# One copy of each node's row for both experts, in two row buffers, with the weight picked in the block

## The chip, the core and the metric

One core of a Trainium2 chip runs the whole kernel in one launch. The metric is the time of one execution on the device in microseconds (us), as a median of several runs. The engines are named as in the profile: PE (matmul; PEld is its weight load), DVE (vector), ACT (scalar/activation), POOL (GpSimd, which issues the gathers and scatters), and SP (SyncE, which issues the plain DMAs).

## The reference

The input is 6250 nodes of 256 features and 100000 edges of 96 features, sorted by target node `dst`. The kernel computes two layers, each with a residual around it:

```
x = x + gnn(layernorm(x))
    gnn(v): sums, maxima and means of the edges of each node
            h = relu(concat[v, sum, max, mean, u] @ W1 + b1) @ W2 + b2;  return h + v
x = x + ffn(layernorm(x))
    ffn(v): gate_logits = v @ gate_w + gate_b            # 16 experts
            the two best experts, weights softmax(their logits)
            each: relu(v @ w1[e] + b1[e]) @ w2[e] + b2[e]
            y = v + weighted sum;  return layernorm(y) * gamma + beta
```

## The kernel before

Node tiles have P = 125 nodes; there are 50, taken from the last to the first in 13 groups: group 0 has two tiles, the others four (GS = 4). The order of all work is written out by hand: `at_slot(T, function, ...)` puts a function at a slot, the slots are run through in order, and each engine gets its instructions in that order. A group has 12 slots (SLOTS); B = 12 g is the first slot of group g. Between the slots a stream of edge work (`steps`, lines 316 to 320) is laid on DVE by a time budget of 4.6 us a slot.

**First stage, by group.** For group g: edge rows are gathered by POOL (`take_edges` L722 and `take_carry` L729, from about slot B - 10), joined on DVE (`join_edges`, L735 and L737), masked on ACT (`mask_edges`, L742), turned on PE (`turn`, L755, copied out by ACT L756), and put through the MLP (`hidden` L766 and L771, `output` L779, eight slots and four slots). DVE adds the residual (`residual`, L784) and takes statistics. `find_block` and `take_blocks` (L490 to L495) find the edges' places by gathers of POOL. `chain_runs` carries runs over partitions on DVE (L395, L396, L438) and POOL writes them (`carry_d`, L440).

**Routing of a group.** `root_b` and `scale_b` give the scale of the second layer norm (`stat`); `norm_b` at slot B + 15 writes the normalized rows into the tile `xr` on ACT (L806); `turn_b` turns them on PE (L818), `logits` L826, `choose`, `rank` and `place` (slot B + 22) give each node its two experts, its two places in the row store `xg_d`, and its two weights; `send` (slots B + 23 and B + 24, two tiles each) scatters the rows with POOL's indirect DMA (L891), two DMAs a tile, eight a group. Each row has 256 features and 5 more numbers (DR = D + 5): its weight, the node with a mark for the later of the two, the place of the partner row, and the two numbers that undo the layer norm. `xr` holds two copies of each row, since weight, mark and partner differ, and there is one buffer of it (`xrp`, bufs=1).

**Last stage, by block.** A block is 256 rows of one expert. The first NA = 14 blocks are of one often chosen expert whose full blocks are known early; then `count_all` and `table_rest` work out the others, 43 blocks (b = 14 to 56). `load_block` (SP) loads the rows xb, the expert's weights wt (1026 KB) and its output bias eb, three buffers of weights, issued two blocks ahead. `run_block(b)` orders one block as follows: `weigh(b-1)` (DVE L1053 adds pY and xe to yb; ACT L1055 scales it by the row's weight; SP stores it in `y_d`), the load of b + 2, `finish(b-2)` (DVE L1093, L1094, then POOL's scatter L1096), the first half of the first matmuls (L1122, ACT L1128), `turn_block(b+1)` (PE L1036, copy xT, DVE L1041 for xe, and for b >= NA the indices from_i L1044 and to_i L1046), the second half, POOL's gather of the partner rows (`take_partners`, L1066), `stats_y(b-1)` (L1074 to L1089), and the second matmuls (L1142). The scale for a row is read straight from the loaded row:

```
nc.scalar.activation(yb[:, h, :], yb[:, h, :], AF.Copy, scale=xb[:, h, D:D + 1])
```

Of the kernel before, what the change touches and what calls it, by code (L numbers as in the profile page):

```python
# [9 lines left out]
F32 = mybir.dt.float32  # L10
# [9 lines left out]
P = 125  # L20
# [10 lines left out]
GS = 4  # L31
# [13 lines left out]
def kernel(  # L45
# [35 lines left out]
    WROW = B1O + FC  # L81
    NR = (2 * N - NE) // SB + NE
    NB = NA + NR
    DR = D + 5
    NG = (NT + GS - 1) // GS
    ER = EP * sum(JR)

# [104 lines left out]
    gtp = mlp.enter_context(tc.tile_pool(name="gt", bufs=2))  # L192
    sm = mlp.enter_context(tc.tile_pool(name="sm", bufs=2))
    xrp = mlp.enter_context(tc.tile_pool(name="xr", bufs=1))
    win0 = ExitStack()
    w0p = win0.enter_context(tc.tile_pool(name="win0", bufs=2))
    EP_ = {}
# [602 lines left out]

    def norm_b(g):
        a, z = GRP[g]
        G[g]["xr"] = xr = xrp.tile([P, GS, 2, DR], F32, name="xr")
        for i in range(z - a):
            t = a + i
            nc.scalar.activation(xr[:, i, :, 0:D], G[g]["xt"][:, i, None, :].to_broadcast([P, 2, D]), AF.Identity,  # L806
                                 scale=stat[:, 0, t:t + 1], bias=stat[:, 1, t:t + 1])
        n = z - a
        nc.scalar.copy(xr[:, :n, :, D + 3], stat[:, 2, a:z, None].to_broadcast([P, n, 2]))
        nc.scalar.copy(xr[:, :n, :, D + 4], G[g]["mvb"][:, :n, 0:1].to_broadcast([P, n, 2]))  # L810

    def turn_b(g, k):
        n = GRP[g][1] - GRP[g][0]
        if k == 0:
            G[g]["gT"] = gtp.tile([128, DC, GS * P], F32, name="gT", bufs=1)
        pT = pTp.tile([128, GS * P], F32, name="pT")
        for i in range(n):
            nc.tensor.transpose(pT[:, i * P:(i + 1) * P], G[g]["xr"][:, i, 0, k * 128:(k + 1) * 128], ident[:P, :P])  # L818
        nc.scalar.copy(G[g]["gT"][:, k, :n * P], pT[:, :n * P])

    def logits(g):
# [42 lines left out]
    def place(g):  # L864
        a, z = GRP[g]
        n, xr, mk, dv = z - a, G[g]["xr"], G[g]["mk"], G[g]["dv"]

        rk = gtp.tile([P, GS, NE], F32, name="rk")
        nc.vector.tensor_tensor(rk[:, :n], G[g]["pR"][:, :n * NE].rearrange("p (i e) -> p i e", e=NE),
                                erow[:, None, :].to_broadcast([P, n, NE]), op=OP.add)  # L870
        nc.vector.tensor_tensor(mk[:, :n], mk[:, :n], rk[:, :n, None, :].to_broadcast([P, n, 2, NE]), op=OP.mult)
        posf = gtp.tile([P, GS, 2], F32, name="posf")
        nc.vector.tensor_reduce(posf[:, :n], mk[:, :n], AX.X, OP.add)
        G[g]["pos"] = pos = xrp.tile([P, GS, 2], I32, name="pos_i", bufs=2)
        nc.vector.tensor_copy(pos[:, :n], posf[:, :n])

        w0 = gtp.tile([P, GS], F32, name="w0")
        nc.vector.tensor_scalar(w0[:, :n], dv[:, :n], 1.0, None, op0=OP.add)
        nc.vector.reciprocal(w0[:, :n], w0[:, :n])
        nc.vector.tensor_copy(xr[:, :n, 0, D], w0[:, :n])  # L880
        nc.vector.tensor_mul(xr[:, :n, 1, D], w0[:, :n], dv[:, :n])
        last = gtp.tile([P, GS, 2], F32, name="i2")
        nc.vector.tensor_tensor(last[:, :n], posf[:, :n, ::-1], posf[:, :n], op=OP.is_gt)
        nc.vector.scalar_tensor_tensor(xr[:, :n, :, D + 1], last[:, :n], float(2 * N),
                                       node_i[:, a:z, None].to_broadcast([P, n, 2]), op0=OP.mult, op1=OP.add)
        nc.vector.scalar_tensor_tensor(xr[:, :n, :, D + 2], last[:, :n], float(NE * N), posf[:, :n, ::-1],  # L886
                                       op0=OP.mult, op1=OP.add)

    def send(g, i):
        for k in range(2):  # L890
            d = nc.gpsimd.indirect_dma_start(out=xg_d[:, :],  # L891
                                             out_offset=IndirectOffsetOnAxis(ap=G[g]["pos"][:, i, k:k + 1], axis=0),
                                             in_=G[g]["xr"][:, i, k, :], in_offset=None)
# [26 lines left out]
    def open_experts():  # L920
        edges_until(len(JR) - 1)
        assert next(stream, None) is None
        edges.close()
        MB["pools"] = pools = ExitStack()
        for nm, bufs in (("tb", 1), ("wp", 3), ("xg", 6), ("bk", 3), ("yb", 4)):
            MB[nm] = pools.enter_context(tc.tile_pool(name=nm, bufs=bufs, side="right"))
        tb = MB["tb"]
        MB["half"] = half = tb.tile([128, 2], F32, name="half_i")
        nc.gpsimd.iota(half, pattern=[[-2 * N, 2]], base=0, channel_multiplier=-4 * N, allow_small_or_imprecise_dtypes=True)
        MB["tab_a"] = tb.tile([1, NA], I32, name="tab_a")  # L930
        MB["tab"] = tb.tile([1, 2, NR], I32, name="tab")
        MB["seen"] = tb.tile([128, NR], F32, name="seen")
        MB["more"] = tb.tile([1, 1], I32, name="more")
# [64 lines left out]
    def table_rest_2():  # L998
        pe = eps.tile([1, 2, NR], F32, name="ps")
        for k in range(2):  # L1000
            nc.tensor.matmul(pe[:, k, :], MB["er"][:, k:k + 1], ident[:NR, :NR], start=True, stop=True)
        nc.vector.tensor_copy(MB["tab"], pe)
        ps = pGp.tile([128, NR], F32, name="pg")
        nc.tensor.matmul(ps, MB["skip"].to_broadcast([NR, 128]), ident[:NR, :NR], start=True, stop=True)
        nc.vector.tensor_scalar(MB["seen"], ps, float(2 * N), None, op0=OP.mult)

    def open_final():
        mlp.close()
# [22 lines left out]
    def turn_block(b):  # L1031
# [7 lines left out]
        copy(xT, pX.rearrange("p k h r -> p k (h r)"))  # L1039
        BL[b]["xe"] = xe = MB["bk"].tile([128, 2, D], F32, name="xe")  # L1040
        nc.vector.tensor_tensor(xe, xb[:, :, 0:D], BL[b]["eb"][:, None, :].to_broadcast([128, 2, D]), op=OP.add)  # L1041
        if b >= NA:
            BL[b]["from"] = from_i = MB["xg"].tile([128, 2], I32, name="from_i")
            nc.vector.tensor_copy(from_i, xb[:, :, D + 2])  # L1044
            BL[b]["to"] = to_i = MB["xg"].tile([128, 2], I32, name="to_i")
            nc.vector.scalar_tensor_tensor(to_i, MB["half"], MB["seen"][:, b - NA:b - NA + 1], xb[:, :, D + 1],  # L1046
                                           op0=OP.add, op1=OP.max)

    def weigh(b):

        xb, xe = BL[b]["xb"], BL[b]["xe"]
        BL[b]["yb"] = yb = MB["yb"].tile([128, 2, D], F32, name="yb")
        nc.vector.tensor_tensor(yb, BL[b]["pY"], xe, op=OP.add)  # L1053
        for h in range(2):
            nc.scalar.activation(yb[:, h, :], yb[:, h, :], AF.Copy, scale=xb[:, h, D:D + 1])  # L1055
        r = BL[b]["r"]
        d = nc.sync.dma_start(y_d[ds(r, SB), :].rearrange("(p h) d -> p h d", h=2), yb.bitcast(I32))
        tc.declare_no_dep(d.ins, group="taken", reason="rows taken so far were written by earlier blocks")
# [13 lines left out]
    def stats_y(b):  # L1072
# [7 lines left out]
            nc.vector.bn_aggr(mv[:, h, :], bs)  # L1080
        BL[b]["z"] = z = MB["gy"].tile([128, 2, D], F32, name="z", bufs=3)
        for h in range(2):
            nc.scalar.activation(z[:, h, :], xb[:, h, 0:D], AF.Identity, scale=xb[:, h, D + 3:D + 4], bias=xb[:, h, D + 4:D + 5])
# [75 lines left out]
    def at_slot(T, fn, *a, cost=0.0):  # L1159
        tasks.append((T, len(tasks), fn, a, cost))  # L1160
# [21 lines left out]
    for g, (a, z) in enumerate(GRP):  # L1182
# [79 lines left out]

    def fill_rows():

        nc.vector.memset(fill[:, D + 1:], float(NE * N))
# [41 lines left out]
    cut_x = windows_of(xrp.tile([P, GS, 2, DR], F32, name="xr").rearrange("p i k d -> p (i k d)"), 1)[0]  # L1307
# [185 lines left out]
```

## Time and profile before

| | before |
|---|---|
| runs, median | 1313.23 us (1313.06, 1313.23, 1322.8) |
| profiled execution | 1304.08 us, span 1302.3 us |
| PE, PEld busy | 1134.1 us (87%), 788.7 us (61%) |
| DVE, ACT, POOL busy | 929.0 (71%), 646.4 (50%), 591.3 us (45%) |
| mean granted clock of PE | 0.947 |
| DMA | 260.99 MB, 200 GB/s |

| stretch, us | PE | DVE | ACT | POOL | clock | DMA share |
|---|---|---|---|---|---|---|
| 400 to 500 (groups) | 84.13 | 84.84 | 55.27 | 56.22 | 0.93 | 0.89 |
| 600 to 700 (groups) | 94.59 | 91.83 | 39.76 | 50.25 | 0.93 | 0.90 |
| 700 to 822 (groups, no edges left) | 120.09 | 54.30 | 47.54 | 40.11 | 1.00 | 0.31 |
| 822 to 900 (first blocks) | 74.15 | 32.52 | 21.57 | 17.07 | 0.98 | 0.25 |
| 1000 to 1100 (blocks) | 95.02 | 69.51 | 67.75 | 59.08 | 1.00 | 0.75 |
| 1100 to 1200 (blocks) | 97.85 | 71.51 | 69.76 | 58.04 | 1.00 | 0.77 |

The columns of the second table are busy microseconds in the stretch. The first activation of `norm_b` starts at 145.9, 205.2, 274.6, 327.5, 395.1, 462.7, 520.3, 579.1, 634.0, 692.3, 740.4, 789.7 and 835.4 us for groups 0 to 12. The first transposes of block 0 are at 820.50, those of block 14 at 937.65, of block 56 at 1265.51.

How to read the lines that follow. A line of the waits reads: engine, written tile and line, the releaser after the arrow, then the total wait in us, how often, and the longest. A line of a timeline reads: start in us, duration, engine, line, operation, written tile and read tiles, shapes, count, and in brackets the idle time of the engine before it with what ended it. In the slices each digit is the busy share of a fortieth of the span in tenths.

### The profile page before, as it was taken

The page shows a single profiled execution, that of the slowest core. Times are in us where ns is not written, and L with a number is a line of the kernel's source. Part 1 is how long each engine was busy: PE and PEld are TensorE (multiplying, and loading weights), DVE is VectorE, ACT ScalarE, POOL GpSimd, SP SyncE. Part 2 cuts the span into 40 slices and gives each one's busy share as a digit, 9 for nine tenths or more (in the row PEclk, how much of TensorE's full clock was granted, in tenths as well). Part 3 has the DMA queues.
Part 4 walks back from the last instruction along what each step waited for, and adds up shares of the span by engine and source line. Part 5 has one row for each costly group of instructions (what it writes and reads, how often), then busy time and mean ns, then how long its engine had stood idle before and what let it go on. Part 6 is the DMA issues. An engine that isn't in the chain of part 4 may idle for free.

```text
span 1302.3 us, 16684 instructions
## 1 busy us (share of the span) xinstructions
PE 1134.1 (87%) x4631; PEld 788.7 (61%) x4631; DVE 929.0 (71%) x2465; ACT 646.4 (50%) x1484; POOL 591.3 (45%) x731
## 2 busy tenths in 40 slices
PE   2494899879888879999999999997999999999992
PEld 1262365536545444646465565886888888888882
DVE  4569888869996989989999441444347767776764
ACT  3394256444637452533435333221266766676663
POOL 4122254563466654383643450303046656555664
PEclk9897799889998989989989999998999999999997
DMA  5948876795888897879988311222366777878771
GB/s 161 217 103 237 212 231 183 202 273 149 237 213 260 230 289 192 245 202 257 262 245 241 105 50 62 65 66 81 120 230 223 257 253 262 278 246 270 268 271 70
DMA packets 179473, 260.99 MB, mean 200 GB/s; under 512 B 35915, under 2 KB 145963, under 8 KB 173729
## 3 DMA queue, kind: packets, MB, share of 16 engines
q1 hardware_dynamic: 140241, 202.11, 52.0%
q0 software_dynamic: 39008, 57.22, 15.5%
q8 instruction: 40, 0.66, 0.2%
q14 instruction: 72, 0.59, 0.1%
q10 hardware_dynamic: 112, 0.41, 0.1%
HBM read 146.59 MB, written 121.88 MB: 206 GB/s over the span
## 4 chain that ended last, share of the span: by engine, by line
PE 30%; DMA 8%; DVE 7%; issue 3%; ACT 3%; SPq 2%; POOL 2%; DVEq 0%; POOLq 0%; ACTq 0%
PE acc L1122 9%; PE acc L1142 9%; PE acc L771 6%; DMA eb<-in_eb_dram 5%; PE acc L779 3%; POOL xg_d L891 1%; DMA xt<-in_x_dram 1%; DVE yb L1053 1%; PE pT L1036 1%; ACT yb L1055 1%; DMA rows_d<-rw 1%; DVE bsc L1079 1%; DMA cg<-carry_d,next_i 1%; DVE z L1089 1%; ACT hb L1128 1%
## 5 line engine op out<-in xcount | busy, mean ns | idle before, releaser
L771 PE MATMUL acc<-inT,w1x 128*128 128x500 f32 (+1 forms) x832 | 374.3, 601 | 0.0
L771 PEld LDWEIGHTS acc<-inT,w1x 128*128 128x128 f32 x832 | 162.7, 203 | 184.1 <-issue 182.2
L891 POOL DMA_INDIRECT xg_d<-xr,pos_i x100 | 133.4, 1334 | 241.1 <-DVE xr L886 177.6
L1122 PE MATMUL acc<-xT,wt 128*128 128x256 f32 x912 | 223.9, 389 | 15.2 <-ACT hb L1128 13.6
L1142 PE MATMUL acc<-wt,hb 128*128 128x256 f32 x912 | 206.8, 380 | 0.0
L1122 PEld LDWEIGHTS acc<-xT,wt 128*128 128x128 f32 x912 | 169.8, 192 | 45.9 <-ACT hb L1128 23.0
L1142 PEld LDWEIGHTS acc<-wt,hb 128*128 128x128 f32 x912 | 173.9, 191 | 23.9
L779 PE MATMUL acc<-w2s,hT 128*125 128x256 f32 x800 | 183.6, 386 | 0.0
L773 ACT ACTIVATE hT<-acc,c 128x500 f32<-128x500 f32 (+1 forms) x104 | 68.5, 658 | 226.2 <-PE acc L771 226.0
L779 PEld LDWEIGHTS acc<-w2s,hT 128*125 128x125 f32 x800 | 150.7, 192 | 22.8 <-issue 0.9
L1096 POOL DMA_INDIRECT out_dram<-g,to_i x86 | 95.7, 1113 | 104.2 <-ACT xT L1039 73.0
L1066 POOL DMA_INDIRECT g<-y_d,from_i x86 | 89.9, 1046 | 88.4 <-DVE to_i L1046 51.8
L495 POOL DMA_INDIRECT gb<-in_dst_dram,blk_i x50 | 67.9, 1359 | 131.1 <-DVE blk_i L492 77.6
L1128 ACT ACTIVATE hb<-acc,wt 128x256 f32<-128x256 f32 x200 | 87.9, 465 | 51.7 <-PE acc L1122 51.7
L1055 ACT ACTIVATE yb<-yb,xb 128x256 f32<-128x256 f32 x114 | 51.7, 501 | 103.1 <-DVE yb L1053 101.7
L316 DVE TENSOR_TENSOR rw<-rw,keep 125x768 f32<-125x768 f32 x81 | 77.2, 953 | 11.3 <-DMA rows_d<-rw 9.8
L319 DVE TENSOR_TENSOR rw<-rw,raw 125x768 f32<-125x768 f32 x88 | 83.4, 948 | 0.3 <-DMA raw<-in_edge_dram 0.3
L320 DVE TENSOR_TENSOR rw<-rw,raw 125x768 f32<-125x768 f32 x88 | 83.6, 950 | 0.0
L317 DVE TENSOR_TENSOR rw<-rw,bar 125x768 f32<-125x768 f32 x81 | 82.1, 1013 | 0.0
L756 ACT COPY inT<-pT 128x500 f32<-128x500 f32 (+1 forms) x65 | 35.9, 553 | 89.6 <-PE pT L755 89.5
L722 POOL DMA_INDIRECT at<-rows_d,first_i x44 | 62.5, 1420 | 37.6 <-issue 19.0
L1041 DVE TENSOR_TENSOR xe<-xb,eb 128x512 f32<-128x512 f32 x57 | 39.4, 691 | 55.7 <-DMA eb<-in_eb_dram 55.7
(301 smaller groups left out, 1633.5 us busy)
## 6 DMA issues: line engine op xcount, KB each, us to landing
wt<-in_wpack_dram SPq DMA_DIRECT2D x44, 1026.0 KB
rows_d<-rw SPq DMA_DIRECT2D x46, 960.0 KB
rows_d<-rw SPq DMA_DIRECT2D x46, 540.0 KB
raw<-in_edge_dram SPq DMA_DIRECT2D x46, 480.0 KB
xb<-xg_d SPq DMA_DIRECT2D x57, 261.0 KB
y_d<-yb SPq DMA_DIRECT2D x57, 256.0 KB
raw<-in_edge_dram SPq DMA_DIRECT2D x46, 270.0 KB
xt<-in_x_dram SPq DMA_DIRECT2D x12, 500.0 KB
```

The costliest lines, as they stand in the source:

```text
L316: nc.vector.tensor_tensor(su, prev[0], keep[c][:, :, s + j, None].to_broadcast(bcast), op=OP.mult)
L317: nc.vector.tensor_tensor(mx, prev[1], bar[c][:, :, s + j, None].to_broadcast(bcast), op=OP.min)
L319: nc.vector.tensor_tensor(su, su, x_j, op=OP.add)
L320: nc.vector.tensor_tensor(mx, mx, x_j, op=OP.max)
L771: nc.tensor.matmul(pH[:, :n * P], w1x[:, k, ms], inT[:, k, :n * P], start=False, stop=(k == KC - 1))
L779: nc.tensor.matmul(pO, G[g]["hT"][m][:, i * P:(i + 1) * P], w2s[:, m, :], start=(m == 0), stop=(m == HC - 1))
L891: d = nc.gpsimd.indirect_dma_start(out=xg_d[:, :], out_offset=IndirectOffsetOnAxis(ap=G[g]["pos"][:, i, k:k + 1], axis=0), in_=G[g]["xr"][ ...
L1066: d = nc.gpsimd.indirect_dma_start(out=g[:, h, :].bitcast(I32), out_offset=None, in_=y_d[:, :], in_offset=IndirectOffsetOnAxis(ap=BL[b]["f ...
L1096: d = nc.gpsimd.indirect_dma_start(out=out[:, :], out_offset=IndirectOffsetOnAxis(ap=BL[b]["to"][:, h:h + 1], axis=0), in_=g[:, h, :], in_ ...
L1122: nc.tensor.matmul(pB[i][:, half, :], wt[:, k * FF + m * 128:k * FF + (m + 1) * 128], xT[:, k, :], start=(k == 0), stop=(k == DC - 1))
L1128: nc.scalar.activation(hb[:, m, :], pB[i][:, half, :], AF.Relu, bias=bias)
L1142: nc.tensor.matmul(pY[:, h, :], hb[:, m, h * 128:(h + 1) * 128], wt[:, W2O + m * D:W2O + (m + 1) * D], start=(m == order[0]), stop=(m == o ...
```

## The change

A row gets 7 more numbers instead of 5, the same for both experts: both weights (D, D + 1), the second place (D + 2), the sum of both places (D + 3), the node (D + 4), and the two numbers of the layer norm. Both sends of a tile take the same copy. The tile holds two groups, `xr2[:, g % 2]`. The block works out by itself which weight is its own: it compares the second place with the row's own place (`at`, a table made once from the block table by one more pair of matmuls and an addition), gets the partner's place as sum minus own, and from the order of the two the mark that was sent before. In the first 14 blocks, whose expert has the lowest places, a comparison with N is enough. The sends of groups 0 to 9 are put one slot later. All places of the cleared rows are set to a larger number so that the new arithmetic leaves them out.

```diff
-    DR = D + 5
+    DR = D + 7
...
+    xr2 = xrp.tile([P, 2, GS, DR], F32, name="xr")
...
     def norm_b(g):
-        G[g]["xr"] = xr = xrp.tile([P, GS, 2, DR], F32, name="xr")
+        G[g]["xr"] = xr = xr2[:, g % 2]
         for i in range(z - a):
-            nc.scalar.activation(xr[:, i, :, 0:D], G[g]["xt"][:, i, None, :].to_broadcast([P, 2, D]), AF.Identity,
+            nc.scalar.activation(xr[:, i, 0:D], G[g]["xt"][:, i, :], AF.Identity,
                                  scale=stat[:, 0, t:t + 1], bias=stat[:, 1, t:t + 1])
-        nc.scalar.copy(xr[:, :n, :, D + 3], stat[:, 2, a:z, None].to_broadcast([P, n, 2]))
-        nc.scalar.copy(xr[:, :n, :, D + 4], G[g]["mvb"][:, :n, 0:1].to_broadcast([P, n, 2]))
+        nc.scalar.copy(xr[:, :n, D + 4], node_i[:, a:z])
+        nc.scalar.copy(xr[:, :n, D + 5], stat[:, 2, a:z])
+        nc.scalar.copy(xr[:, :n, D + 6], G[g]["mvb"][:, :n, 0])
...
     def place(g):
-        w0 = gtp.tile([P, GS], F32, name="w0")
-        nc.vector.tensor_scalar(w0[:, :n], dv[:, :n], 1.0, None, op0=OP.add)
-        nc.vector.reciprocal(w0[:, :n], w0[:, :n])
-        nc.vector.tensor_copy(xr[:, :n, 0, D], w0[:, :n])
-        nc.vector.tensor_mul(xr[:, :n, 1, D], w0[:, :n], dv[:, :n])
-        last = gtp.tile([P, GS, 2], F32, name="i2")
-        nc.vector.tensor_tensor(last[:, :n], posf[:, :n, ::-1], posf[:, :n], op=OP.is_gt)
-        nc.vector.scalar_tensor_tensor(xr[:, :n, :, D + 1], last[:, :n], float(2 * N), ...)
-        nc.vector.scalar_tensor_tensor(xr[:, :n, :, D + 2], last[:, :n], float(NE * N), ...)
+        w0, w1 = xr[:, :n, D], xr[:, :n, D + 1]
+        nc.vector.tensor_scalar(w1, dv[:, :n], 1.0, None, op0=OP.add)
+        nc.vector.reciprocal(w0, w1)
+        nc.vector.tensor_mul(w1, w0, dv[:, :n])
+        nc.vector.tensor_copy(xr[:, :n, D + 2], posf[:, :n, 1])
+        nc.vector.tensor_add(xr[:, :n, D + 3], posf[:, :n, 0], posf[:, :n, 1])
...
     def send(g, i):
-                                             in_=G[g]["xr"][:, i, k, :], in_offset=None)
+                                             in_=G[g]["xr"][:, i, :], in_offset=None)
...
     def table_rest_2():
-        ps = pGp.tile([128, NR], F32, name="pg")
-        nc.tensor.matmul(ps, MB["skip"].to_broadcast([NR, 128]), ident[:NR, :NR], start=True, stop=True)
+        ps = pGp.tile([128, 2, NR], F32, name="pg")
+        for k, of in enumerate((MB["skip"], MB["er"][:, 1:2])):
+            nc.tensor.matmul(ps[:, k], of.to_broadcast([NR, 128]), ident[:NR, :NR], start=True, stop=True)
+        nc.vector.tensor_tensor(MB["at"], ps[:, 1, :, None].to_broadcast([128, NR, 2]),
+                                MB["pair"][:, None, :].to_broadcast([128, NR, 2]), op=OP.add)
...
     def turn_block(b):
-        if b >= NA:
-            BL[b]["from"] = from_i = MB["xg"].tile([128, 2], I32, name="from_i")
-            nc.vector.tensor_copy(from_i, xb[:, :, D + 2])
-            BL[b]["to"] = to_i = MB["xg"].tile([128, 2], I32, name="to_i")
-            nc.vector.scalar_tensor_tensor(to_i, MB["half"], MB["seen"][:, b - NA:b - NA + 1], xb[:, :, D + 1],
-                                           op0=OP.add, op1=OP.max)
+        w0, w1, pos1, both, node = (xb[:, :, D + k] for k in range(5))
+        BL[b]["w"] = w = MB["xg"].tile([128, 2], F32, name="w_b")
+        if b < NA:
+            nc.vector.scalar_tensor_tensor(w, pos1, float(N), w1, op0=OP.is_ge, op1=OP.add)
+            nc.vector.tensor_tensor(w, w, w0, op=OP.min)
+            return
+        own = MB["at"][:, b - NA]
+        nc.vector.tensor_tensor(w, pos1, own, op=OP.not_equal)
+        nc.vector.tensor_add(w, w, w1)
+        nc.vector.tensor_tensor(w, w, w0, op=OP.min)
+        other, late = (MB["xg"].tile([128, 2], F32, name=nm) for nm in ("other", "late"))
+        nc.vector.tensor_sub(other, both, own)
+        nc.vector.tensor_tensor(late, other, own, op=OP.is_gt)
+        BL[b]["from"] = from_i = MB["xg"].tile([128, 2], I32, name="from_i")
+        nc.vector.scalar_tensor_tensor(from_i, late, float(NE * N), other, op0=OP.mult, op1=OP.add)
+        nc.vector.scalar_tensor_tensor(late, late, float(2 * N), node, op0=OP.mult, op1=OP.add)
+        BL[b]["to"] = to_i = MB["xg"].tile([128, 2], I32, name="to_i")
+        nc.vector.scalar_tensor_tensor(to_i, MB["half"], MB["seen"][:, b - NA:b - NA + 1], late, op0=OP.add, op1=OP.max)
...
     def weigh(b):
-            nc.scalar.activation(yb[:, h, :], yb[:, h, :], AF.Copy, scale=xb[:, h, D:D + 1])
+            nc.scalar.activation(yb[:, h, :], yb[:, h, :], AF.Copy, scale=BL[b]["w"][:, h:h + 1])
...
-            at_slot(B + SLOTS + 11 + i // 2, send, g, i)
+            at_slot(B + SLOTS + (12 if g < NG - 3 else 11) + i // 2, send, g, i)
```

More of the change, by code (lines that the diff above doesn't have):

```diff
@@ L817, in turn_b @@
         for i in range(n):
-            nc.tensor.transpose(pT[:, i * P:(i + 1) * P], G[g]["xr"][:, i, 0, k * 128:(k + 1) * 128], ident[:P, :P])
+            nc.tensor.transpose(pT[:, i * P:(i + 1) * P], G[g]["xr"][:, i, k * 128:(k + 1) * 128], ident[:P, :P])
         nc.scalar.copy(G[g]["gT"][:, k, :n * P], pT[:, :n * P])
@@ L875, in place @@
         nc.vector.tensor_copy(pos[:, :n], posf[:, :n])
-        w0 = gtp.tile([P, GS], F32, name="w0")
-        nc.vector.tensor_scalar(w0[:, :n], dv[:, :n], 1.0, None, op0=OP.add)
-        nc.vector.reciprocal(w0[:, :n], w0[:, :n])
-        nc.vector.tensor_copy(xr[:, :n, 0, D], w0[:, :n])
-        nc.vector.tensor_mul(xr[:, :n, 1, D], w0[:, :n], dv[:, :n])
-        last = gtp.tile([P, GS, 2], F32, name="i2")
-        nc.vector.tensor_tensor(last[:, :n], posf[:, :n, ::-1], posf[:, :n], op=OP.is_gt)
[L884 to L887, printed above, removed]
+        w0, w1 = xr[:, :n, D], xr[:, :n, D + 1]
[4 more added lines that the diff above has]
+        nc.vector.tensor_add(xr[:, :n, D + 3], posf[:, :n, 0], posf[:, :n, 1])
     def send(g, i):
@@ L931, in open_experts @@
         MB["tab"] = tb.tile([1, 2, NR], I32, name="tab")
+        MB["pair"] = pair = tb.tile([128, 2], F32, name="pair_i")
+        nc.gpsimd.iota(pair, pattern=[[1, 2]], base=0, channel_multiplier=2, allow_small_or_imprecise_dtypes=True)
         MB["seen"] = tb.tile([128, NR], F32, name="seen")
+        MB["at"] = tb.tile([128, NR, 2], F32, name="at_row")
         MB["more"] = tb.tile([1, 1], I32, name="more")
@@ L1002, in table_rest_2 @@
         nc.vector.tensor_copy(MB["tab"], pe)
-        ps = pGp.tile([128, NR], F32, name="pg")
-        nc.tensor.matmul(ps, MB["skip"].to_broadcast([NR, 128]), ident[:NR, :NR], start=True, stop=True)
-        nc.vector.tensor_scalar(MB["seen"], ps, float(2 * N), None, op0=OP.mult)
+        ps = pGp.tile([128, 2, NR], F32, name="pg")
+        for k, of in enumerate((MB["skip"], MB["er"][:, 1:2])):
+            nc.tensor.matmul(ps[:, k], of.to_broadcast([NR, 128]), ident[:NR, :NR], start=True, stop=True)
+        nc.vector.tensor_scalar(MB["seen"], ps[:, 0], float(2 * N), None, op0=OP.mult)
+        nc.vector.tensor_tensor(MB["at"], ps[:, 1, :, None].to_broadcast([128, NR, 2]),
+                                MB["pair"][:, None, :].to_broadcast([128, NR, 2]), op=OP.add)
     def open_final():
@@ L1041, in turn_block @@
         nc.vector.tensor_tensor(xe, xb[:, :, 0:D], BL[b]["eb"][:, None, :].to_broadcast([128, 2, D]), op=OP.add)
-        if b >= NA:
-            BL[b]["from"] = from_i = MB["xg"].tile([128, 2], I32, name="from_i")
-            nc.vector.tensor_copy(from_i, xb[:, :, D + 2])
-            BL[b]["to"] = to_i = MB["xg"].tile([128, 2], I32, name="to_i")
-            nc.vector.scalar_tensor_tensor(to_i, MB["half"], MB["seen"][:, b - NA:b - NA + 1], xb[:, :, D + 1],
-                                           op0=OP.add, op1=OP.max)
+        w0, w1, pos1, both, node = (xb[:, :, D + k] for k in range(5))
[16 more added lines that the diff above has]
+        nc.vector.scalar_tensor_tensor(to_i, MB["half"], MB["seen"][:, b - NA:b - NA + 1], late, op0=OP.add, op1=OP.max)
     def weigh(b):
-        xb, xe = BL[b]["xb"], BL[b]["xe"]
+        xe = BL[b]["xe"]
         BL[b]["yb"] = yb = MB["yb"].tile([128, 2, D], F32, name="yb")
@@ L1082, in stats_y @@
         for h in range(2):
-            nc.scalar.activation(z[:, h, :], xb[:, h, 0:D], AF.Identity, scale=xb[:, h, D + 3:D + 4], bias=xb[:, h, D + 4:D + 5])
+            nc.scalar.activation(z[:, h, :], xb[:, h, 0:D], AF.Identity, scale=xb[:, h, D + 5:D + 6], bias=xb[:, h, D + 6:D + 7])
         nc.scalar.activation(rs, mv[:, :, 1], AF.Sqrt, bias=eps_t)
@@ L1263, in fill_rows @@
     def fill_rows():
-        nc.vector.memset(fill[:, D + 1:], float(NE * N))
+        nc.vector.memset(fill[:, D + 1:], 4.0 * NE * N)
         for h in range(SB // 128):
@@ L1306 @@
     w1u = wk.tile([P, GS, D], F32, name="xn", bufs=1).rearrange("p i d -> p (i d)")[:GF, 0:HID]
-    cut_x = windows_of(xrp.tile([P, GS, 2, DR], F32, name="xr").rearrange("p i k d -> p (i k d)"), 1)[0]
+    cut_x = windows_of(xr2.rearrange("p k i d -> p (k i d)"), 1)[0]
     cut_w = w2s[:P].rearrange("p k d -> p (k d)")[:, 0:WE * EF].rearrange("p (k f) -> p k f", f=EF)
```

## The prediction

> **What bounds the kernel now.** Each view in turn. First the page's slices: which engine is full where.
>
> ```profile
> PE   2494899879888879999999999997999999999992
> DVE  4569888869996989989999441444347767776764
> DMA  5948876795888897879988311222366777878771
> ```
>
> A slice is 32.6 us. Up to slice 21 (700 us) DVE and PE are both nearly full: DVE folds edges, PE runs the node MLP. From 700 to 822 PE is alone and full (118.99 of 120 us at clock 1.00). From 905 to 1290 the 43 blocks of the chosen experts run, with PE, DVE and DMA all busy. The change touches the first stage and the last, so I priced each by itself.
>
> Second, the list of waits, for the step that the change rebuilds and for what runs next to it.
>
> ```profile
> DVE xe L1041 <- DMA eb<-in_eb_dram: 55.7, 36, 3.7
> DVE yb L1053 <- PE acc L1142: 52.2, 39, 2.9
> DVE at L735 <- DMA cg<-carry_d,next_i: 37.7, 10, 10.3
> PE pT L818 <- ACT xr L806: 30.0, 18, 10.3
> ACT xr L806 <- DMA at<-rows_d,first_i: 26.9, 3, 13.3
> ```
>
> L806 is norm_b's first activation of a group. With one buffer it cannot write before the eight row sends (L891) of the group before have landed; the releaser printed is only the DMA that came last by the records. The starts of L806 show real waits of ACT in groups 2, 4, 5, 6 and 9: 9.5, 11.2, 13.3, 2.3 and 4.0 us, and PE, whose transposes L818 follow, idles 6.5, 8.2, 10.3, 0 and 1.0 us.
>
> Third, the timelines of group 5's stall and of what came after it.
>
> ```profile
> 453.42 1.43 POOL L891 DMA_INDIRECT xg_d<-xr,pos_i  x1 [0.21 <-issue]
> 462.71 2.93 ACT L806 ACTIVATE xr<-xt,stat 125x512 f32<-125x512 f32 x4 [13.29 <-DMA at<-rows_d,first_i]
> 463.57 0.47 PE L818 MATMUL pT<-ident,xr 125*128 125x125 f32 x1 [10.27 <-ACT xr L806]
> 466.07 1.44 POOL L729 DMA_INDIRECT cg<-carry_d,next_i  x1 [0.30 <-issue]
> 474.56 3.48 DVE L735 SCALAR_TENSOR_TENSOR at<-cg,cross,at 125x96 f32<-125x96 f32 x1 [4.66 <-DMA cg<-carry_d,next_i]
> 488.13 0.44 ACT L742 ACTIVATE at<-at,ne_n 125x192 f32<-125x192 f32 x1
> 488.24 0.71 PE L755 MATMUL pT<-ident,at 125*128 125x125 f32 x4
> ```
>
> Read downwards: PE loses 10.3 us at 463, but at 488.24 it needs the edge sums of group 7, and these come just then, from the mask on ACT (488.13) after the join on DVE (474.56) after a gather on POOL (466.07) that stands in POOL's queue behind gathers and sends. Groups 4 and 6 meet in the same way (L755 at 299.96 with a wait of 0.69 on L742; at 421.35, beside the last L742 at 421.10). So PE's stall is slack against the join, and POOL's queue plus DVE set the end of the stage. The residual adds (L784) say the same: in groups 2 to 9 they start 3 to 12 us after PE has finished (L779), so DVE is the late one.
>
> Last, a block of the last stage.
>
> ```profile
> 1023.95 0.69 DVE L1041 TENSOR_TENSOR xe<-xb,eb 128x512 f32<-128x512 f32 x1 [1.19 <-DMA eb<-in_eb_dram]
> 1024.56 0.16 DVE L1044 CAST from_i<-xb 128x2 int32<-128x2 f32 x1
> 1024.63 0.22 DVE L1046 SCALAR_TENSOR_TENSOR to_i<-half_i,seen,xb 128x2 int32<-128x2 f32 x1
> 1024.76 0.69 DVE L1074 TENSOR_TENSOR g<-yb,g 128x512 f32<-128x512 f32 x1
> 1028.28 0.69 DVE L1053 TENSOR_TENSOR yb<-acc,xe 128x512 f32<-128x512 f32 x1 [0.30 <-PE acc L1142]
> 1056.53 0.69 DVE L1041 TENSOR_TENSOR xe<-xb,eb 128x512 f32<-128x512 f32 x1 [3.59 <-DMA eb<-in_eb_dram]
> 1060.48 0.68 DVE L1053 TENSOR_TENSOR yb<-acc,xe 128x512 f32<-128x512 f32 x1
> 1062.52 0.70 PE L1122 MATMUL acc<-xT,wt 128*128 128x256 f32 x2 [1.99 <-ACT hb L1128]
> ```
>
> An undisturbed block takes PE 7.53 us. DVE waits for eb, runs a chain of 3.95 us at least from xe to the next yb, and then is ready 0.30 us before PE's product: almost no slack. When eb lands late (1056.53) yb is late, ACT's scaling and hb stand behind it, and PE stalls for 1.99 us (1062.52 is yb + 2.04, as in the blocks around). This is where a longer DVE chain hurts.
>
> **The change, part by part.**
>
> *Two row buffers.* In the built order norm_b's first activation of a group waited on all eight semaphores of POOL's DMA queue; now it waits for DVE's statistics, and its activations for lanes of sends two groups back, which landed some 50 us before. So the five waits go, 40.3 us of ACT and 26.0 us of PE. What is late next is the join, at the three places above: PE would arrive some 10 us early and wait there. On the path I count only what the join itself gains: the carry write, which moves ahead of the last four sends in two groups, ends a 2.3 us wait of DVE at 275 (L395), the gathers behind a lane may leave 1.5 us sooner at 274, and L490 waits 1.4 us at 407 for an ACT that stood behind L806. These partly overlap: -2 us; bounds 0, and -26.0 with the half-rate time below if PE were the bound after all. Group 9 comes after the last gather wait: -1.0 us.
>
> The row on the clock: in 450 to 472, around group 5's stall, PE was granted 0.77 of its clock, in 385 to 410 0.73, in 265 to 285 0.83, against 1.00 from 700 to 820. I estimate some 8 us of PE time lost at half rate after the three stalls.
> [...]
>
> *Sends one slot later.* On POOL only the two carry writes change place. The second one waits for ct of L438, ready at 318.0, while the fourth send ends near 313.6: the last four sends and the gathers behind them start up to 4 us later. Joins of that group follow at 345.8, so cover is there; without it, 4 us. Counted 0.
>
> *place.* From pos_i (876.97) to the end of L886 (878.24) DVE took 1.27 us for seven small operations; the five that are left, at 0.19 us from start to start where one needs the other and 0.08 where not, end 0.48 us sooner. DVE is the late engine up to group 10: 11 x 0.48 = -5.3 us; bounds 0 (all reabsorbed by gathers) and -6.2 (13 groups).
>
> *norm_b on ACT.* 50 activations of 0.80 us become ones of 256 columns, 0.59 by L706's row: 10.5 us less, one more small copy of 0.19 a group. ACT is 40 to 57% busy there and nobody waits but L818: 0; without that cover -0.8 us a group.
>
> *Blocks.* Between xe and g stand two small operations (0.20 us); now eight, seven of them in dependent runs: 0.20 + 0.20 + 0.08 + five of 0.20 + 0.13 us against 0.20. The start-to-start of dependent small operations is that of L993 to L918, 0.18 to 0.24 us. So +1.2 us (bounds 0.6, if they start 0.08 apart, and 1.4).
> [...]
>
> In 40 blocks (b = 17 to 56) DVE's slack before yb ranges from 0 (12 blocks) to 0.9 us and adds up to 20.2 us. Delays add up to 40 x 1.2 - 20.2 = 27.8 us. A late yb(b-1) holds back, through SP's queue (y_d store, then xb, wt and eb for b+2), the eb that yb(b+1) needs: the loop spans two blocks, so a delay is paid once per two: +13.9 us. Bounds +4 (0.6 us) and +27.8 (paid in each block). Behind the delayed yb stand ACT's scaling and hb, hence PE; take_partners has from_i a block ahead of need.
>
> *Star blocks, table, bytes.* Two operations in each of 14 blocks: DVE waits 2.6 to 2.9 us for PE there: 0; without that, 0.28 each. One more pair of matmuls (0.31) and an addition (about 0.25) before the table's yb: +0.6. Rows of 8 bytes more: 0.1% of 261 MB: 0.
>
> **Sum:** -2 - 1.0 - 5.3 + 13.9 + 0.6 = +6.2 us. The profiled execution took 1304.08 us (span 1302.3), so 1310.3 by it; the runs' median is 1313.23, 9 us above it, and I add the same difference: **1319.4 us**, +0.5%. Differences under 1% (13 us) can hardly be told from none by these runs.
>
> **The rivals.**
> A: the waits pay in full. For: 26.0 us of idle PE and the clock. Against: the join rows. -26 - 8 in place of -3 and -5.3, blocks +14.5: 1293.7 us, 1.5% faster.
> B, on the slower side: the delayed yb is paid in each block, not in every second. It decides once eb lands over 10.0 us after yb(b-3), as in nearly all 40 blocks, and when each block's load also waits on its neighbour. For: SP's queue is in order. Against: an undisturbed DVE round is 6.0 + 1.2 = 7.2 us, under 7.53. +27.8 + 0.6 - 8.3: 1333.3 us, 1.5% slower.
> C: it doesn't do what it says, norm_b still waits (for lanes shared with later gathers). The built order speaks against it. -5.3 + 14.5: 1322.4 us.
>
> **How the numbers follow.** Forecast 0.47, A 0.14, B 0.33, C 0.06. Forecast and C lie within 1%: 0.53; A gives faster 0.14, B slower 0.33. The range goes from 1300 (join gains a third of PE's waits) to 1335 (B with its bound), leaving most of A out.
>
> **What would show it.** Right: L806's waits on DMA gone, PE's idle time moved before L755 or L766, the span up to block 0 about 8 us shorter, about 1.2 us more from xe to g, and block pitch up by some 0.35 us. Wrong: block 0 over 20 us earlier (A), a mean pitch over 8.3 us (B), or L806 still waiting (C).

## The result, and the profile after

The changed kernel takes 1330.5 us (median of 17 runs, 1323.8 to 1342.4); the kernel before takes 1313.1 us on the same chips (17 runs, 1305.5 to 1322.8). The ratio is 1.015, 95% interval 1.0124 to 1.0177: 1.5% slower, some 17 to 20 us. The forecast was 1319.4 us with a range of 1300 to 1335, so the time lies in the range, but the loss is about three times the +6.2 us of the sum and near the price of rival B.

Each kernel was profiled twice. The table gives the start of three additions yb on VectorE (L1053 before, L1068 after): block 0 is the end of the first stage, 16 to 56 are the blocks that the prediction summed over.

| | time of that execution | yb of block 0 | yb of block 16 | yb of block 56 | 16 to 56 | mean pitch |
|---|---|---|---|---|---|---|
| before | 1304.08 | 830.3 | 966.8 | 1281.3 | 314.5 | 7.86 |
| before, again | 1310.66 | 830.3 | 968.5 | 1288.3 | 319.7 | 7.99 |
| after | 1332.15 | 827.9 | 965.9 | 1309.9 | 343.9 | 8.60 |
| after, again | 1332.27 | 831.0 | 968.1 | 1310.2 | 342.1 | 8.55 |

The first profile of before comes from an execution 9 us under its median, and both of after lie 2 us above theirs, so the difference between the profiles (25 us on average) is larger than that of the medians. The picture is plain all the same: the first stage ends where it did, within the 3 us by which two profiles of one kernel differ, and everything is lost in 40 blocks.

The page's slices of the changed kernel, to be laid beside those of before:

```profile
PE   2494899879896969799999999998998998988883
DVE  4569889879986989899987414444487777777675
DMA  5948868785988897978995231122666767767762
```

In the last ten slices, which are blocks, PE shows 8 in six where before had 9 in all but the last, and DVE 7 nearly throughout where before had 7 and 6: more VectorE work per block, and a PE that waits.

The list of waits of the changed kernel, with the idle us, the times and the longest:

```profile
DVE yb L1068 <- PE acc L1157: 40.2, 24, 3.2
DVE at L736 <- DMA cg<-carry_d,next_i: 37.7, 9, 12.8
PE acc L1137 <- ACT hb L1143: 34.0, 32, 3.0
DVE xe L1044 <- DMA eb<-in_eb_dram: 31.4, 26, 4.0
PE pg L862 <- DVE mm L853: 25.5, 6, 10.5
```

Three things are to be seen. norm_b's wait on a DMA (L807 now) is gone from the list, and PE's 30.0 us ahead of its transposes with it; but 25.5 us stand at L862, the next place where PE needs VectorE. VectorE's wait for PE ahead of yb has shrunk from 52.2 us in 39 blocks to 40.2 in 24: its slack is used up. And PE now waits 34.0 us for hb in 32 blocks (13.6 in 14 before).

Group 5 in the changed kernel's timelines, first PE's line, then VectorE's, then PE's again:

```profile
457.01 0.59 PE L820 MATMUL pT<-ident,xr 125*128 125x125 f32 x4
476.08 2.60 DVE L736 SCALAR_TENSOR_TENSOR at<-cg,cross,at 125x96 f32<-125x96 f32 x1 [4.01 <-issue]
488.23 0.22 DVE L853 TENSOR_TENSOR mm<-mk 125x64 f32<-125x64 f32 x1
488.50 0.68 PE L862 MATMUL pg<-mm,before 125*125 125x64 f32 x2 [10.47 <-DVE mm L853]
489.60 0.63 PE L756 MATMUL pT<-ident,at 125*128 125x125 f32 x2
```

PE transposes group 5's rows at 457.0, where before it waited until 463.6. Then it runs dry 10.47 us long, because rank's mask (L853) stands in VectorE's queue behind the join (L736), which is no earlier than before (476.08 against 474.56). The transposes of the edge sums start at 489.60; before it was 488.24. The stall of 10.3 us has become one of 10.5 us, 25 us later.

A late block in VectorE's timeline and the matmuls of PE that follow:

```profile
1242.42 0.69 DVE L1044 TENSOR_TENSOR xe<-xb,eb 128x512 f32<-128x512 f32 x1 [4.01 <-DMA eb<-in_eb_dram]
1243.03 0.15 DVE L1052 TENSOR_TENSOR w_b<-xb,at_row 128x2 f32<-128x2 f32 x1
1244.27 0.22 DVE L1062 SCALAR_TENSOR_TENSOR to_i<-half_i,seen,late 128x2 int32<-128x2 f32 x1
1244.41 0.69 DVE L1089 TENSOR_TENSOR g<-yb,g 128x512 f32<-128x512 f32 x1
1247.55 0.68 DVE L1068 TENSOR_TENSOR yb<-acc,xe 128x512 f32<-128x512 f32 x1
1249.58 3.66 PE L1137 MATMUL acc<-xT,wt 128*128 128x256 f32 x8 [3.03 <-ACT hb L1143]
```

From xe to yb it is 5.13 us with no idle time but 0.36 us for the root (the square root that ScalarE takes); that is the shortest chain of the changed kernel, against 3.95 before. PE's product had been ready since 1243.9, and PE starts its second half 2.03 us after yb, after a stall of 3.03 us. Its eight matmuls then take 3.66 us where an undisturbed block takes 1.99. The windows around them say why (us of the window, busy times of PE, PEld, DVE, ACT and POOL, the granted clock, DMA share, GB/s):

```profile
1249.50:1252.90 3.40, 3.32 (x8) 2.66 (x9) 3.12 (x14) 1.35 (x4) 2.27 (x3) 0.51 0.43 147
1252.90:1257.00 4.10, 4.10 (x21) 3.61 (x20) 1.70 (x7) 2.73 (x6) 2.52 (x6) 0.99 0.86 274
```

For 3.4 us after the stall PE was granted half its clock. Blocks 16 to 56 of before had no such window in either profile.

**Where the time of a block goes.** In every profile, PE's second half starts 2.04 us after the yb before it, the last matmul of the product 5.08 us later and the next yb at the earliest 0.41 us later: 7.53 us. What a block takes beyond this is one of three things, which can be read off block by block: VectorE is still busy when PE's product is ready; or VectorE is idle and PE's release comes late all the same; or the 5.08 us are longer, at half clock. Added up from yb 16 to yb 56 (0 stands for less than 0.6; where a yb is late for both of the first two reasons, the split between them is good to some 0.6 us in a sum):

| kernel | 16 to 56 | PE, 40 x 7.53 | VectorE late | PE's release late | half clock |
|---|---|---|---|---|---|
| before; again | 314.5; 319.7 | 301.2 | 13.4; 18.8 | 0; 0 | 0; 0 |
| after; again | 343.9; 342.1 | 301.2 | 29.3; 31.6 | 8.7; 0 | 4.6; 9.1 |
| one buffer | 347.2 | 301.2 | 32.5 | 4.2 | 9.0 |
| small operations before xe | 322.0 | 301.2 | 18.2 | 1.1 | 1.2 |
| loads before store | 305.5 | 301.2 | 2.2 | 1.1 | 0 |
| both; again | 303.7; 303.5 | 301.2 | 2.4; 2.2 | 0 | 0 |
| before, six operations more | 331.5 | 301.2 | 23.1 | 4.4 | 2.7 |
| before, twelve operations more | 367.8 | 301.2 | 53.9 | 0 | 12.7 |
| before, loads first; again | 303.5; 303.5 | 301.2 | 2.2; 2.2 | 0 | 0 |

The 2.2 to 2.4 us of VectorE in the last rows are one block, the last, which is as late in nearly every profile. The 1.1 us in the row of the loads before the store are late releases inside two blocks, 34 and 48, at clock 1.00.

### The profile page after: what moved, and what is told of

Its sections match the earlier page's. It is cut to its first block, busy times and chain, and to the rows that moved or that the text cites. A ratio compares the mean times of both kernels' runs of the same rounds, so it can differ in the third digit from the quotient of the medians.

```text
span 1330.3 us, 16956 instructions
## 1 busy us (share of the span) xinstructions
PE 1136.9 (85%) x4633; PEld 796.3 (60%) x4633; DVE 970.2 (73%) x2726; ACT 637.4 (48%) x1497; POOL 589.1 (44%) x732
## 4 chain that ended last, share of the span: by engine, by line
PE 24%; DVE 11%; DMA 9%; issue 4%; ACT 3%; SPq 3%; POOL 0%; DVEq 0%; POOLq 0%; ACTq 0%
PE acc L1157 8%; PE acc L1137 8%; DMA eb<-in_eb_dram 5%; PE acc L772 4%; PE acc L780 3%; DMA rows_d<-rw 3%; DVE yb L1068 2%; ACT yb L1070 1%; DMA xt<-in_x_dram 1%; ACT hb L1143 1%; SPq L176 1%; DVE z L1104 1%; DVE rw L321 1%; DVE bsc L1094 1%; DVE g L1089 1%
## 5 line engine op out<-in xcount | busy, mean ns | idle before, releaser
L772 PE MATMUL acc<-inT,w1x 128*128 128x500 f32 (+1 forms) x832 | 365.4, 590 | 0.0
L772 PEld LDWEIGHTS acc<-inT,w1x 128*128 128x128 f32 x832 | 159.1, 198 | 178.4 <-issue 176.0
L1137 PE MATMUL acc<-xT,wt 128*128 128x256 f32 x912 | 229.2, 396 | 35.8 <-ACT hb L1143 34.0
L1137 PEld LDWEIGHTS acc<-xT,wt 128*128 128x128 f32 x912 | 172.7, 195 | 69.5 <-ACT hb L1143 45.3
L780 PE MATMUL acc<-w2s,hT 128*125 128x256 f32 x800 | 189.7, 395 | 0.0
L780 PEld LDWEIGHTS acc<-w2s,hT 128*125 128x125 f32 x800 | 155.5, 198 | 24.6 <-issue 0.9
L1070 ACT ACTIVATE yb<-yb,w_b 128x256 f32<-128x256 f32 x114 | 51.8, 501 | 100.1 <-DVE yb L1068 98.5
L723 POOL DMA_INDIRECT at<-rows_d,first_i x44 | 62.2, 1413 | 33.3 <-PE acc L772 16.1
L1068 DVE TENSOR_TENSOR yb<-acc,xe 128x512 f32<-128x512 f32 x57 | 39.2, 688 | 48.5 <-PE acc L1157 40.2
```

The lines of the kernel that those rows point to most:

```text
L772: nc.tensor.matmul(pH[:, :n * P], w1x[:, k, ms], inT[:, k, :n * P], start=False, stop=(k == KC - 1))
L780: nc.tensor.matmul(pO, G[g]["hT"][m][:, i * P:(i + 1) * P], w2s[:, m, :], start=(m == 0), stop=(m == HC - 1))
L1137: nc.tensor.matmul(pB[i][:, half, :], wt[:, k * FF + m * 128:k * FF + (m + 1) * 128], xT[:, k, :], start=(k == 0), stop=(k == DC - 1))
```

## The experiments

**Small operations ahead of xe.** The block picks its weight and places while VectorE waits for eb.

```diff
-        nc.vector.tensor_tensor(xe, xb[:, :, 0:D], eb ..., op=OP.add)
         w, other, late, from_i, to_i: eight operations on 128 x 2
+        nc.vector.tensor_tensor(xe, xb[:, :, 0:D], eb ..., op=OP.add)
```

> The changed kernel with one thing moved: in each block of the chosen experts the eight small VectorE operations (w_b, other, late, from_i, to_i) stand ahead of xe, where VectorE waits for eb anyway, and no longer between xe and g. Theory (position): what costs is the chain from xe to the next yb, 5.13 us at the shortest in the changed kernel against 3.95 before. With all eight in front of xe the chain falls to about 3.75, the small operations hide in the wait for eb, and the blocks run as before or better: 40 blocks give back the 29 us that the two profiles differ by in blocks 16 to 56, the runs come to 1305 to 1313 us, and the mean pitch of the blocks returns to 7.8 us or less. Rival (sum of work): VectorE's round per block, about 1.2 us longer, costs wherever it stands; 1326 to 1332 us and a pitch near 8.5. Second rival (not the small operations: the scale of yb from w_b, longer rows, the clock): unchanged, 1328 to 1333 us.

Measured: 1308.3 us (12 runs, 1302.3 to 1316.3) against 1309.1 of before, ratio 0.9997 (0.9974 to 1.002). The shortest chain is 3.74 us, VectorE's lateness 18.2 us, and its wait for eb 18.9 us in place of 31.4: the operations went into it. VectorE does the same work per block as in the changed kernel, so it is the place that costs, not the sum; that rival and the one that blamed something else fall.

**The six operations alone, on the kernel before**, and twelve of them. They write a tile that nobody reads.

```diff
             nc.vector.scalar_tensor_tensor(to_i, ...)
+            more = MB["xg"].tile([128, 2], F32, name="more_b")
+            nc.vector.tensor_copy(more, xb[:, :, D + 2])
+            for _ in range(5):        # 11 in the run with twelve
+                nc.vector.tensor_add(more, more, xb[:, :, D])
```

> The kernel before with six dependent small VectorE operations on a 128 x 2 tile that nobody reads, put behind to_i in each block of the chosen experts; nothing else is changed, so the rows, the buffers, the sends and place are those of before. It prices the block part alone. The prediction's term (a delay is paid once per two blocks) gives +13.9 us: 1327 us, mean pitch of blocks 16 to 56 near 8.2. Rival B (paid in each block) gives +27.8: 1341 us, pitch near 8.55. If something else of the change is the cost (the weight tile that yb's scaling reads, rows of 8 bytes more), the time stays at 1311 to 1316 us.

> The kernel before with twelve small VectorE operations behind to_i in each block in place of six. Six lengthened the shortest chain from xe to yb by 1.07 us and the runs by 16.5 us. The step in dispute is how often a delay is paid. Twelve lengthen the chain by about 2.2 us. If the recurrence over two blocks holds (once per two blocks, and the rest where VectorE's round of 6.0 + 2.2 = 8.2 us passes PE's 7.53), it gives +37 us: 1344 to 1350 us, pitch near 8.8. Paid in each block (rival B): 40 x 2.2 - 20.2 = 68 us: 1372 to 1380 us, pitch near 9.5. If cost went with the number of operations alone, at the rate of the six: +33 us, 1342 us.

Measured: six, 1325.9 us, ratio 1.0126 (1.0094 to 1.0159), chain 5.01 us at the shortest. So six operations whose result nobody uses cost nearly what the whole change costs. Twelve: 1361.8 us, ratio 1.0382 (1.0337 to 1.0427), chain 6.17 us. Over the 1309.1 us of before that is +16.8 and +52.6 us, and both lie between the forecast's rule (+13.9; +37) and rival B's (+27.8; +68). The table parts them: with twelve, VectorE's lateness grew by 37.8 us over the mean of before (53.9 less 16.1). The prediction's rule gives (40 x 2.23 - 20.2) / 2 = 34.5 us for a chain 2.23 us longer, and the expectation's 37 us counted the rounds over 7.53 us besides; the other 12.7 us are PE at half clock. With six, the lateness grew by 7.0 us where the rule gives (40 x 1.07 - 20.2) / 2 = 11.3, with 7.1 us of the other two terms: one execution, and here the shares do not fit. So the rule "paid once per two blocks" fits VectorE's lateness with twelve operations and overrates it with six, and what the block times have above it is half clock and late releases.

**Loads ahead of the store on SP's queue.**

```diff
     def run_block(b, end):
-        run_due("weigh", weigh, 0)            # ends with the store of yb(b-1)
         if b + 2 < end and "wt" not in BL[b + 2]:
             load_block(b + 2)
+        run_due("weigh", weigh, 0)
```

> The changed kernel with the order on SP's queue turned round in each block: the loads of block b+2 (xb, wt, eb) are issued ahead of the store of yb(b-1), which stands first in both kernels and waits for VectorE and ScalarE. Theory (loop): eb is late because its load stands behind that store, issued 1.66 us after yb begins; with the loads in front, they wait for PE's last product alone and eb lands some 1.6 us sooner, more than the 1.2 us that the small operations add. Then the waits of xe for eb shrink, the loop is cut and the time falls to 1305 to 1316 us, pitch 7.6 to 7.9. Rival (bandwidth): eb lands when the 1 MB of wt ahead of it has been moved, at 220 to 250 GB/s in these stages; an earlier issue only queues, and the time stays within 1326 to 1332 us. Gathers of y_d may be later by the three issues, about 1 us, which should not show.

Measured: 1298.8 us (12 runs), ratio 0.9944 (0.9919 to 0.9968), 0.6% faster than before, with the small operations where the change put them. VectorE no longer waits for eb at all, and PE's wait for hb is almost gone. From the list of waits of this kernel:

```profile
DVE yb L1068 <- PE acc L1157: 52.1, 49, 4.9
PE acc L1137 <- ACT hb L1143: 3.5, 5, 2.1
```

The loop is shown, and the rival that eb only waits for bandwidth falls. But the 1.6 us of the expectation were wrong. SP's own queue in the timelines shows the gain, first in the kernel before, around the yb of 1028.28, then in this one:

```profile
1029.94 0.35 SPq L1057 DMA_DIRECT2D y_d<-yb  x1
1032.53 0.33 SPq L1027 DMA_DIRECT2D wt<-in_wpack_dram  x1
1033.05 0.33 SPq L1029 DMA_DIRECT2D eb<-in_eb_dram  x1
```

```profile
1105.94 0.33 SPq L1030 DMA_DIRECT2D wt<-in_wpack_dram  x1
1106.47 0.33 SPq L1032 DMA_DIRECT2D eb<-in_eb_dram  x1
1107.52 0.36 SPq L1072 DMA_DIRECT2D y_d<-yb  x1
```

Before, eb is issued 4.76 us after yb (median of 39 blocks): 1.66 us to the store, 1.98 us in which SP loads the block's expert and row from the table (L1018, L1019) and issues xb, then wt and eb. With the loads in front, wt goes out as soon as PE has done the product (0.09 us after yb) and eb 0.61 us after yb: 4.15 us sooner. What stood behind the store was not one issue but SP's register loads as well.

**One row buffer in the changed kernel.**

```diff
-        G[g]["xr"] = xr = xr2[:, g % 2]
+        G[g]["xr"] = xr = xr2[:, 0]
```

> The changed kernel with both groups in the same row buffer, so that norm_b's first activation waits again for the sends of the group before. It prices the second buffer alone; the sends, place and the blocks are those of the changed kernel. The prediction's term (the join sets the pace): waits of ScalarE of 4 to 13 us are back in groups 2, 4 and 5, and the time is only 3 us longer, 1331 to 1335 us. Rival A (PE's waits were on the path): 26 to 34 us longer, 1355 to 1365 us. Second rival: the longer wait is hidden altogether, 1328 to 1332 us.

Measured: 1331.4 us (6 runs), ratio to before 1.0159 (1.0115 to 1.0203), where the changed kernel has 1.015. The waits are all back, in the list of waits of this kernel:

```profile
ACT xr L807 <- DMA xg_d<-xr,pos_i: 35.2, 10, 11.0
PE pT L820 <- ACT xr L807: 25.7, 8, 8.5
PE pg L862 <- DVE mm L853: 13.9, 5, 3.6
```

and yb of block 0 starts at 827.6 us, against 827.9 and 831.0 with two buffers. 25.7 us of an idle PE cost nothing that can be seen: rival A, with its 26 to 34 us, falls. The two ratios differ by 0.1%, with an uncertainty of 0.5%, so the second buffer is worth about 1 us, give or take 7.

**The loads first on the kernel before, and both edits on the changed one.** The diffs are those above.

> The kernel before with the order on SP's queue turned round (xb, wt and eb of block b+2 issued ahead of the store of yb(b-1)); nothing else is changed. It asks whether the gain of the same edit on the changed kernel comes from the loop alone. Theory (the loop through SP's queue is the limit of the blocks in both kernels): PE's stalls ahead of the second half of the hidden layer, 11.5 us in the profile of before, go to about 1 us, as they did in the changed kernel (35.8 to 1.0 us), the pitch of blocks 16 to 56 falls from 7.86 to 7.6, and the time by 8 to 12 us: 1297 to 1302 us. Rival (the edit only repairs what the longer chain broke; before has enough slack): 1307 to 1311 us.

> The changed kernel with both edits: small operations ahead of xe, and the loads ahead of the store. With the loads in front PE has only 1.0 us of stall left in the blocks, so by the loop theory the place of the small operations is worth nothing more: 1295 to 1301 us, within 3 us of the run with the loads alone. Rival (the two add up, since the chain is 1.4 us shorter): 1288 to 1293 us, which would need a pitch under PE's own 7.53 us. Second rival: small operations in front delay xe, since xb arrives no earlier than eb; 1300 to 1308 us.

Measured: before with the loads first 1295.5 us, ratio 0.9885 (0.9854 to 0.9915); after with both edits 1292.7 us, ratio 0.9867 (0.9837 to 0.9897). The blocks take 303.5 and 303.7 us in the two, pitch 7.59: PE's own pace. So the loop limited the blocks of the kernel before too, by 11 to 16 us, and the time came out 1.5 us under the lowest that was expected. The changed kernel with both edits is 6 us below the one with the loads alone, measured on another chip, where at most 3 us were expected; the blocks of the two profiles account for 2 us of it, and the rest stays open. The rival's 1288 to 1293 us is touched, but not for its reason: the pitch is 7.59, not under 7.53.

**Each kernel once more for its profile.**

> The kernel before once more, unchanged, for a second profile: it tells how far the stage up to the blocks and the stage of the blocks move from one execution to the next. The first profile had block 0's yb at 830.3 us and a pitch of 7.86 in blocks 16 to 56. Theory that the first profile was a quick execution of the blocks: pitch 7.9 to 8.1, block 0 at 829 to 834. If it was typical: pitch 7.83 to 7.9.

> The changed kernel once more, unchanged, for a second profile of its blocks. In all ten profiles so far the time from yb of block 16 to yb of block 56 is the sum of four terms to within 0.3 us: 40 x 7.53 = 301.2 of PE; yb late because VectorE is late (before 13.4 and 18.8, changed 29.3, with one buffer 32.5); yb late though VectorE is idle and PE's last product is done by the records (before 0, changed 8.7, with one buffer 4.2); PE at half its clock after a stall of over 2.5 us (before 0, changed 4.6, with one buffer 9.0). Theory: the first term is what the small operations cost by themselves, and it comes near 29 to 33 again; the other two are what stalls bring with them, and they move from one execution to the next: 2 to 9 us each. Then the stage takes 335 to 350 us. Rival: the late release of PE belonged to one execution alone; that term is under 1 us, and the stage takes under 336 us.

Measured: before again 1310.7 us, yb of block 0 at 830.3 again, pitch 7.99; the first profile was a quick execution of the blocks. After again 1332.3 us: VectorE's lateness 31.6 us as expected, half clock 9.1 us, and no late release of PE at all: the rival is right in that term, which belongs to single executions, while the stage still took 342.1 us. The half clock also came after shorter stalls than the 2.5 us of the expectation, the shortest 1.91 us here and 1.96 us in the first profile of after.

**What the rest of the change is worth.** Both edits with all sends at slot 11 again, and the two kernels without the loop once more, on one chip.

```diff
-            at_slot(B + SLOTS + (12 if g < NG - 3 else 11) + i // 2, send, g, i)
+            at_slot(B + SLOTS + 11 + i // 2, send, g, i)
```

> The changed kernel with both edits (small operations ahead of xe, loads ahead of the store) and with all sends at slot 11 again, as in the kernel before: the part of the change that moves them a slot later is undone. POOL then writes carry_d in two groups behind the last four sends, as before. Prediction's term: 0, so the same time as the next run, within 3 us. Rival: the earlier carry write serves the join, and taking it back costs the 2 to 4 us that the wait of L395 and its gathers show: 2 to 4 us longer than the next run.

> The changed kernel with both edits once more, beside the run above and the run below on the same chip. With the cost of the blocks gone, the difference to the run below is what the rest of the change is worth: two buffers, five operations in place's tail instead of seven, sends later. By the prediction -8.3 us (waits 2, group 9 1.0, place 5.3); by the first yb of the profiles so far (831.2 us on average in five with the changed front, 833.0 in five with the old one) -2 us; by the first pair of runs -2.8 us. 1290 to 1296 us.

> The kernel before with the loads ahead of the store once more, beside the run above: 1293 to 1298 us, 1.1% under the kernel before. If the front of the change is worth what the prediction said, the run above is 0.6% faster than this; if it is hidden behind the joins, 0 to 0.2%.

Measured: sends at slot 11 1291.9 us, ratio to before 0.9858 (0.9814 to 0.9902); both edits 1293.0 us, 0.9863 (0.9822 to 0.9903); before with loads first 1296.5 us, 0.9896 (0.9857 to 0.9935). Moving the sends back changes the time by -0.9 us (difference of the means, standard error 1.5): nothing that can be seen, as the prediction had it. Over both pairs (12 runs each) the changed kernel is 2.85 us faster than the old one once the blocks are equal; the standard error of that difference is 1.04 us, so 0.8 to 4.9 us. With 1292 to 1293 us, 1.3 to 1.4% under the kernel before, the changed kernel with both edits is the fastest that was run, with the sends in either slot.

## Why the prediction was right and wrong, step by step

- **Two buffers: -2 and -1.0 us.** The mechanism was right. L807's waits on DMA are gone, PE's idle time moved instead of going, and the join is where it ends. The place was not: PE waits at L862 for rank's mask, which stands behind the join in VectorE's queue, and not at the L756 that the prediction named, which follows 1.1 us later. The run with one buffer puts the price at about 1 us, give or take 7.
- **place: -5.3 us.** The step that was too large. From pos_i to its end place took 1.08 us before in eleven of the thirteen groups, not the 1.27 of the last two, from which the term was worked out, and it takes 0.80 now: -0.28 us a group, -3 us in eleven. All of the front together, -8.3 us by the sum or -7.7 with the table's 0.6, is worth -2.85 us in the pairs of runs, and yb of block 0 starts at 830.8 us on average in eight profiles with the changed front and at 832.8 in six with the old one (single ones lie from 827 to 838).
- **Sends, ACT, star blocks, table, bytes: +0.6 us.** No run contradicts them; of these, only the sends were tried by themselves.
- **Blocks: +1.2 us of chain.** Measured 1.18 (3.95 to 5.13). The working as written adds up to 1.41 us, since it lists five steps of 0.20; eight operations have four such steps, and with four it gives the 1.2 that was used.
- **Blocks: once per two, +13.9 us.** VectorE's lateness grew from 16.1 to 30.5 us (means of two profiles): +14.4. The term is right for what it prices, and twelve operations bear it out, six do less. The second profile of after shows the two-block loop near its end: blocks 47, 49, 51, 53 and 55 are late by 1.6 to 2.6 us, those between them by 0 to 0.6. What failed is that it was taken for the whole price of the blocks. A PE that waits 2 to 4 us inside a block can pay again, by some 1.7 us where half clock follows (the eight matmuls at 1249.58 took 3.66 us in place of 1.99). In the two profiles of after, half clock adds 4.6 and 9.1 us and late releases 8.7 and 0, together 11 us on average, and the forecast had none of it. The table of before shows PE at clock 1.00 from 1000 to 1200 us, and the prediction counted a clock loss for the first stage alone, where the join covered it.
- **The sum again.** Front -2.9, VectorE late +14.4, half clock +6.9, late release +4.4: +22.8 us. The profiled executions differ by 24.8 us on average, the medians by 17.4. In the second pair of profiles, which is free of late releases, the blocks take 22.4 us longer: 12.8 us of VectorE's lateness and 9.1 us of half clock. Against the forecast, the front's gain was counted 4.9 us too high and half clock at nothing, 6.9 us too low; together 11.8 us, where the median lies 11.1 us above 1319.4.
- **Rival B** named nearly the right time, 1333.3 us, by a mechanism that the table does not show: the lateness is not paid in each block.
- **The signs and the range.** Two of the prediction's signs of being right did not come: up to block 0 the span is some 2 us shorter and not 8, and the pitch rose by 0.65 us (means of two profiles) where 0.35 was forecast. At 8.60 and 8.55 us it passes the 8.3 us that was to show rival B, so that sign cannot tell B from a loss at half clock. The time lies in the range because the range reached up to B's price; the case held likeliest, a difference under 1%, did not come.

In the profiles of after (both), one buffer and twelve operations, all eight stalls of PE over 2.8 us in blocks 16 to 56 were followed by half clock, and so were eleven of the 23 between 1.8 and 2.8 us (from 1.86 us on), some shorter than others that were not (up to 2.69). In the first profile of after, the stalls of 1.96, 2.36 and 3.03 us ahead of L1137 (at 1085.40, 1170.71 and 1249.58) were followed by it, those of 2.08, 2.21 and 2.60 us (at 1222.55, 1268.61 and 1026.08) were not. In these profiles the length of a stall alone does not tell which.

PE's busy time just ahead tells more. By the clock records of that profile the half-clock stretches of blocks 16 to 56 start at 1085.75, 1171.08 and 1249.59, last 3.41 us each and lie 25 and 23 times that length apart. The first profile of after from block 14 to the yb of block 56, cut into lengths of 3.41 us in line with these starts, and that of before in line with its half-clock stretch at 905.40, give 208 lengths. Six of them held at most 1.55 us of PE's work. Three were followed by half clock, with 1.45, 1.05 and 0.38 us; three were not, with 1.53 and 1.55 us (from 1059.00 and 1277.46, before) and 1.45 us (from 1266.65, after). None of the other 202 was. So in these two profiles half clock followed only lengths with little work, and not each of those; what else decides is not shown.

## What to carry to other kernels

Ask of small operations added to a loop not how much work they are but which wait they stand behind: eight of them cost 1.5% after the add that waits for a load (ratio 1.015), and nothing in front of it (0.9997). Where a load is late, read the issuing queue line by line; a store that waits for the end of a chain, issued ahead of loads that don't need it, closed a loop here, and the register loads behind it counted too: eb was issued 4.76 us after yb, 1.98 of them from the store to the next load, and 0.61 us after yb with the loads in front. Where a sum turns slack into stalls, price what a stall itself brings (the clock: 4.6 and 9.1 us in the two profiles of after) in the stage where it falls.

## What was not expected of the hardware

In some blocks yb started late though VectorE was idle and PE's product done by the records, as here in VectorE's timeline of the changed kernel's first profile:

```profile
1049.11 0.69 DVE L1068 TENSOR_TENSOR yb<-acc,xe 128x512 f32<-128x512 f32 x1 [1.50 <-PE acc L1137]
```

PE's last matmul of that product starts at 1047.59, and its semaphore event, 0.39 us after such a start in every block of both profiles of before, comes 1.50 us after it here. It cost 8.7 us in one profile of the changed kernel, 4.2 and 4.4 us with one buffer and with six operations on the kernel before, about 1 us with the small operations first and with the loads first, and nothing in the second profile of the changed kernel. DMA moved 300 to 410 GB/s in those microseconds, as in most blocks without it, and the clock was 1.00.

The traces narrow it down. These five profiles hold 15676 to 16078 recorded semaphore updates; the other nine, which have no late release, hold 18289 to 18756. In four of the five SP too issues eb late, 5.0 to 5.5 us after yb (medians), where all others with the store first have 4.7 to 4.8. One of the five is the kernel before, so the term is not a cost of this change. Four of them ran on one chip; whether the chip, the recording or something else makes it stays open, and no run isolates it.
